# Attention with experts on one core: matrix products in four column groups, another order of the first loads, another router

## The chip, the cores and the metric

The kernel runs on one core of a Trainium2 chip. The metric is the device time of one launch in microseconds, the median of several runs. One further run is recorded by the hardware profiler; its views are called the page (a summary of that execution), the chain of waits (the work that ended last, followed back), the timeline, the groups of instructions and the windows. The engines are called PE (TensorE's matmuls), PEld (its weight loads), DVE (VectorE), ACT (ScalarE), POOL (GpSimd) and SP (SyncE, which here only issues DMAs).

## The reference

Everything is float32. x has the shape (4, 1024, 128): four batches of 1024 tokens of 128 features.

```python
def _L0_attn_ref(x, Wq, Wk, Wv, Wu, rel_bias):       # 8 heads of 16
    ...
    Q, K, V = (silu(Q), silu(K), silu(V))
    scores = jnp.einsum('bhsd,bhtd->bhst', Q, K)
    rel_idx = pos[:, None] - pos[None, :] + MAXLEN - 1
    bias = rel_bias[rel_idx]
    scores = scores + bias.transpose(2, 0, 1)[None]
    scores = scores / jnp.sqrt(jnp.asarray(hd, jnp.float32))
    scores = jnp.where(causal[None, None] == 0, NEG, scores)
    key_mask = jnp.sign(jnp.abs(K).sum(-1))
    scores = jnp.where(key_mask[:, :, None, :] == 0, NEG, scores)
    weights = silu(scores)
    attn = jnp.einsum('bhst,bhtd->bhsd', weights, V)
    ...
    return attn * silu(U)

def _L0_ffn_ref(x, w_gate, w_in, w_out):             # 8 experts, the best 2 are used
    ...
    logits = (xt @ w_gate.T).astype(jnp.float32)
    top_logits, top_idx = jax.lax.top_k(logits, TOP_K)
    top_gates = jax.nn.softmax(top_logits, axis=-1).astype(x.dtype)
    gates = (jax.nn.one_hot(top_idx, E, dtype=x.dtype) * top_gates[..., None]).sum(axis=1)
    for e in range(E):
        h = xt @ w_in[e].T
        y = y + gates[:, e:e + 1] * (h @ w_out[e].T)
    ...

x = x + _L0_attn_ref(_layernorm(x, axis=-1), ...)
x = x + _L0_ffn_ref(_layernorm(x, axis=-1), ...)
```

The weights of attention are silu, not softmax, so no sum over keys is needed. An index of the bias table beyond its end is held at the end, so keys more than 255 tokens back all have the same bias.

## The kernel before

Tokens are handled in blocks of 512 (4 tiles of 128), two a batch, eight in all; the last block is finished in two half groups of 256 tokens. Each step below is a Python generator, and the string ORDER names, letter by letter, which generator takes its next step. No scheduler reorders what follows from it: every engine executes its own instructions in the order in which they were written.

- H, `warm` (L234 to L240): three rounds of products of the identity, whose result is not used.
- K, `constants` (L193): the table `near` of biases by distance, with the causal mask on its diagonal part (L198, L202 on POOL), the far biases copied from `cfar` (L204, on DVE), and small masks.
- P and Q, `prepare` (L289) for the first and the second block of a batch: layernorm, transposed by PE (`layernorm_T`, L255: statistics L262 on DVE, the power L271 and the normalised `xn` L276 on POOL, transposes L283, copy L284). Then keys (L304, with silu into two halves kT, one for even and one for odd heads, L307), queries (L312), the key mask (nz, L318 on DVE, 0/1 products L323, kmask L328), values (L334, silu L339, times the mask L341 on POOL) and the gate U (L351).
- S, `attend` (L355), one unit: scores of 512 columns in all for four pairs of heads (L425), each a product with 32 rows of contraction, in four row groups of the array. DVE adds the near bias (L444), ACT applies silu (L447), or does both for far keys (L452). W, `weigh` (L400), takes the oldest unit that is waiting: products with 128 rows of contraction and 32 output columns (L403), four column groups beside each other, into one accumulator.
- C, D, E, `finish` (L470) for each group of tokens: transposes back (L474), residual, second layernorm, the router's logits (L494, one product a tile: xT is the stationary operand and wgT of 8 columns the moving one; copied out at L496), the choice of the two best and their gates on DVE and POOL (L499 to L534), a transpose of the gates (L542), their way through memory to all partitions (L545, L547 on SP), and gate times x for all experts (L553).
- G, `fold` (L242): w_in and w_out of each expert are multiplied beforehand into one 128x128 matrix (L248).
- X, Y, Z, `experts` (L561): for each tile 8 products accumulated over the experts (L567), residual (L571), store (L607). The last half group uses `experts_then_gates` (L576): products of 512 columns (L585), the gates after.

Except for scores and weighting, a product with a 128x128 stationary operand is one instruction over the whole array (before the compiler's division of each f32 product in two passes). PSUM has a ring of 7 banks (`misc`) and one accumulator for the weighting.

The loads stand at the start (L101 to L148). SP issues both blocks of the first x, the main parts of `near`, `ext` (the bias table with its end repeated, written back to memory, L122), the parts of `near` read from `ext` (L124), the weights of the experts with the other x between. The ACT queue issues the bias table rb, wk, wq, wv, wu, cfar and wgT.

Of the kernel before, what the change touches and what calls it, by code (L numbers as in the profile page):

```python
# [8 lines left out]
F32 = mybir.dt.float32  # L9
BF16 = mybir.dt.bfloat16  # L10
AF = mybir.ActivationFunctionType
# [5 lines left out]
P = 128  # L17
H = 8
# [5 lines left out]
SB = 512  # L24
TPB = SB // P
E = 8
HID = 512
EPS = 1e-5
NEG = -4294967295.0
# [1 line left out]
OFF = -3.0e38  # L31
EULER = 2.718281828459045
RING = 7
LAST = 2


# [2 lines left out]


ORDER = (
    "HHHPPPQQKKKPQPPQQKPQSQKSGGSWSWSGPWPSWWSCPWCSSQWWSCPSQCCPSCWCWPCSCCCWSQGSCWWKCSPPPSWSWSWWCS"
    "WGPSWSWDQSWWSDPGQCWSQQPGQPCCSWSDEQECPPWSQPDSWDWSEGDQEDEDESDWWEDSWQEDSWEWDSXDSWESXSWSWWDSXQ"
    "SEWWSECXECPSWSDEWDWSQPSWDWWDSQYSWWSEEYQPPCSCDSDWCCCESCEWWWCSYQCDSCWSCQYDDCSWWCDWPPQSWSEZQE"
    "SWWSZDCQDSCWDSZCDZCEDDSWDSEEEDWEWSXCSWWCESEWSWSEDDDEXDEXEXDCWDEWSYDCDCCCSCDCCDYCSWDWDCEDDS"
    "CYEYCDSDEEWDWWWDZEEEYYZEZEYEEEEZEYCECCECEEYZYZZZZXZXXX"
)


# [1 line left out]
def preln_silu_attention_moe(  # L51
# [13 lines left out]
    nc = tc.nc  # L65
    B, S, D = x.shape
    NR = rel_biasT.shape[1]
# [15 lines left out]
    def misc():  # L83

        return ps_s.tile([P, SB], F32, tag="bank", name="bank")


    xs = [xpool.tile([P, NT, D], F32, tag="x", name=f"x{b}") for b in range(B)]

# [9 lines left out]
    NPAD = MAXLEN - 1 + TAB  # L99
    FAR = TAB - MAXLEN  # L100
    load_x(0, 0)  # L101
    load_x(0, 1)
    rb = cpool.tile([H, NPAD], F32, tag="rb", name="rb")
    nc.scalar.dma_start(rb[:, NPAD - NR :], rel_biasT)
    wcat = cpool.tile([P, 4, D], F32, tag="wcat", name="wcat")
    for i, w in ((1, wk), (0, wq), (2, wv), (3, wu)):
        nc.scalar.dma_start(wcat[:, i, :], w)
    near = cpool.tile([P, 2, NQ, TAB + P], F32, tag="near", name="near")
    for par in range(2):
        nc.sync.dma_start(  # L110
# [3 lines left out]
                [[1, P], [2 * NR, NQ], [1, MAXLEN]],  # L114
            ),
        )
    nc.vector.tensor_copy(
        rb[:, : NPAD - NR], rb[:, NPAD - NR : NPAD - NR + 1].to_broadcast([H, NPAD - NR])
    )
    gates_d = dpool.tile([B * NB, E, SB], F32, tag="gates_d", name="gates_d")  # L120
    ext = dpool.tile([H, NPAD], F32, tag="ext", name="ext")
    nc.sync.dma_start(ext[:, :], rb)  # L122
    for par in range(2):
        nc.sync.dma_start(  # L124
            near[:, par, :, FAR - P : FAR],
            bass.AP(
                ext.tensor, ext.offset + par * NPAD + FAR - P, [[1, P], [2 * NPAD, NQ], [1, P]]
            ),
        )
    cfar = cpool.tile([P, H], F32, tag="cfar", name="cfar")  # L130
    nc.scalar.dma_start(
        cfar, bass.AP(rel_biasT.tensor, rel_biasT.offset, [[0, P], [NR, H]])
    )
    wgT = cpool.tile([P, E], F32, tag="wgT", name="wgT")
    nc.scalar.dma_start(wgT, w_gateT)
    experts_in = []
    for e0 in range(0, E, 2):
        if e0 in (0, 4):
            load_x(1, e0 // 4)

        if e0 % 4 == 0:
            room = gpool.tile([P, 2, 2, 2, NC, D], F32, tag="wide", name=f"w_in_out_{e0}")
        both = room[:, e0 // 2 % 2]
        for t, w in zip((both[:, 0], both[:, 1]), (w_in, w_outT)):
            nc.sync.dma_start(t, w[e0 : e0 + 2].rearrange("e (c p) d -> p e c d", p=P))
        experts_in.append(both)
    for n in range(2 * NB, B * NB):
        load_x(n // NB, n % NB)  # L148

    def near_of(k, parts):  # L150

# [81 lines left out]

    def warm():  # L234

        for _ in range(3):
            pt = misc()
            for i in range(TPB):
                nc.tensor.matmul(pt[:, i * P : (i + 1) * P], ident, ident, start=True, stop=True)
            yield  # L240

    def fold():  # L242

        for e0, both in zip(range(0, E, 2), experts_in):
            for e in range(2):
                pt = misc()
                for c in range(NC):
                    nc.tensor.matmul(  # L248
                        pt[:, :D], both[:, 0, e, c, :], both[:, 1, e, c, :],
                        start=(c == 0), stop=(c == NC - 1),  # L250
                    )
                nc.scalar.copy(wfold[:, e0 + e, :], pt[:, :D])
                yield
# [35 lines left out]
    def prepare(b, blk):  # L289

        if b not in batches:
            batches[b] = {
                "qT": bpool.tile([P, S], F32, tag="qT", name=f"qT{b}"),
                "kT": bpool.tile([P, 2, S], F32, tag="kT", name=f"kT{b}"),
                "uT": bpool.tile([P, S], F32, tag="uT", name=f"uT{b}"),
                "vp": vps[b % 2],
            }
        qT, kT, uT, vp = (batches[b][n] for n in ("qT", "kT", "uT", "vp"))
        t0 = blk * TPB
        s0 = blk * SB  # L300
        xnT = spool.tile([P, SB], F32, tag="xnT", name="xnT")
        yield from layernorm_T(xs[b][:, t0 : t0 + TPB, :], xnT, "ACT", (b, blk) == (0, 0))
        pt = misc()
        nc.tensor.matmul(pt, wcat[:, 1, :], xnT, start=True, stop=True)  # L304

        for par in range(2):
            nc.scalar.activation(  # L307
                kT[:, par, s0 : s0 + SB], pt, AF.Silu, scale=sel[:, par : par + 1]
            )
        yield  # L310
        pt = misc()
        nc.tensor.matmul(pt, wcat[:, 0, :], xnT, start=True, stop=True)  # L312
        nc.scalar.activation(qT[:, s0 : s0 + SB], pt, AF.Silu)
        yield


        nz = spool.tile([P, SB], BF16, tag="nz", name="nz")
        nc.vector.tensor_tensor(  # L318
            nz, kT[:, 0, s0 : s0 + SB], kT[:, 1, s0 : s0 + SB], ALU.not_equal
        )  # L320
        pt = misc()
        for i in range(TPB):
            nc.tensor.matmul(  # L323
                pt[:, i * H : (i + 1) * H], nz[:, i * P : (i + 1) * P], ones8,
                start=True, stop=True,
            )
        kmask = spool.tile([P, TPB, H], F32, tag="kmask", name="kmask")
        nc.vector.tensor_scalar(  # L328
            kmask.rearrange("p i h -> p (i h)"), pt[:, : TPB * H], 0.0, None, ALU.not_equal
        )  # L330
        yield
        pt = misc()
        for i in range(TPB):
            nc.tensor.matmul(  # L334
                pt[:, i * P : (i + 1) * P], xnT[:, i * P : (i + 1) * P], wcat[:, 2, :],
                start=True, stop=True,
            )
        v = spool.tile([P, TPB, D], F32, tag="v", name="v")
        nc.scalar.activation(v.rearrange("p i d -> p (i d)"), pt, AF.Silu)  # L339
        for par in range(2):  # L340
            nc.gpsimd.tensor_tensor(  # L341
                vp[:, t0 : t0 + TPB, par, :, par, :],
                v.rearrange("p i (k q c) -> p i k q c", k=NQ, q=2)[:, :, :, par, :],
                kmask.rearrange("p i (k q) -> p i k q", q=2)[:, :, :, par]
                .unsqueeze(3)
                .to_broadcast([P, TPB, NQ, HD]),
                ALU.mult,
            )
        yield
        pt = misc()  # L350
        nc.tensor.matmul(pt, wcat[:, 3, :], xnT, start=True, stop=True)  # L351
        nc.scalar.activation(uT[:, s0 : s0 + SB], pt, AF.Silu)
        yield

# [115 lines left out]
    def finish(g, b, t0, nt, gated):  # L470
# [18 lines left out]

        xT = spool.tile([P, nt, P], F32, tag=f"x2T{nt}", name="x2T")  # L490
        yield from layernorm_T(x2, xT.rearrange("p i t -> p (i t)"), "DVE", nt < TPB)
        pt = misc()
        for i in range(nt):
            nc.tensor.matmul(pt[:, i * E : (i + 1) * E], xT[:, i, :], wgT, start=True, stop=True)  # L494
        lg = eight("lg")
        nc.vector.tensor_copy(lg, pt[:, : nt * E].rearrange("p (i e) -> p i e", e=E))  # L496
        yield

        def first_of_largest(v, m, oh, k):  # L499
# [61 lines left out]
    def experts(b, t0, gated):  # L561

        y = spool.tile([P, TPB, D], F32, tag="y", name="y")
        for i in range(TPB):
            pt = misc()
            for e in range(E):
                nc.tensor.matmul(  # L567
                    pt[:, :D], gated[:, e, i * P : (i + 1) * P], wfold[:, e, :],
                    start=(e == 0), stop=(e == E - 1),
                )  # L570
            nc.vector.tensor_tensor(y[:, i, :], pt[:, :D], xs[b][:, t0 + i, :], ALU.add)  # L571
            if i == TPB - 1:
                store(b, t0, TPB, y)
            yield

    def experts_then_gates(b, t0, nt, xT, gates):  # L576
# [3 lines left out]
        for i in range(nt):  # L580
            one = xs[b][:, t0 + i, :]
            gy = spool.tile([P, EH, D], F32, tag="gy", name="gy")
            for e0 in (EH, 0):
                pt = misc()
                nc.tensor.matmul(  # L585
                    pt, xT[:, i, :], wfold[:, e0 : e0 + EH, :].rearrange("p e d -> p (e d)"),
                    start=True, stop=True,
                )
                for e in range(EH):
                    ye = pt[:, e * D : (e + 1) * D]  # L590
# [83 lines left out]
```

## Time and profile before

| what | value |
|---|---|
| median of 4 runs | 291.73 us (291.46 to 291.84) |
| the profiled execution | 291.46 us, of it the span from first to last instruction 289.7 us |
| mean granted TensorE clock | 0.987; 0.5 from 9.2 to 16.1 us after the start |
| first score on PE | 20.39 us |
| start of the last store's work on DVE (L571) | 285.65 us |
| experts' products L567, x448 | 55.1 us busy |
| scores L425, x864, and weighting L403, x864 | 85.6 and 71.9 us busy |
| router L494, x64 | 8.0 us busy |
| moved by DMA | 25.47 MB, 88 GB/s on the mean |

Shares of the span: PE 96%, PEld 55%, DVE 79%, ACT 69%, POOL 36%. The busy time of PE is the time in which some matmul is recorded as under way; matmuls overlap, and their ends are modelled. The starts are the better guide: the chain of waits gives, for each burst of one kind of product, the time until the next burst begins.

### The profile page before, as it was taken

What the parts mean: (1) busy time and instruction counts of PE and PEld (TensorE: products, weight loads), DVE (VectorE), ACT (ScalarE), POOL (GpSimd) and SP (SyncE); (2) the same over time, 40 slices, a digit from 0 to 9 for tenths busy, and PEclk for the clock granted to TensorE, in tenths of its full rate; (3) what the DMA queues carried; (4) which work ended last, traced back from release to release, by engine and by line L of the source; (5) the groups of instructions that cost most, each with busy time, mean ns of one, the idle gap of its engine ahead of it and who ended that gap; (6) DMA issues with size and microseconds to landing.
All of it is one profiled execution on the core that took longest, in us unless ns stands there. A gap on an engine that the chain in (4) does not pass through costs nothing.

```text
span 289.7 us, 6505 instructions
## 1 busy us (share of the span) xinstructions
PE 277.6 (96%) x2591; PEld 160.7 (55%) x2591; DVE 228.7 (79%) x571; ACT 199.2 (69%) x327; POOL 102.9 (36%) x126
## 2 busy tenths in 40 slices
PE   7599999999999999999999999999999999999993
PEld 7255433344445445364653463566676687777873
DVE  3158857688998876879878979887998887797794
ACT  2167999899879778778789787775686683472120
POOL 3812179034207868101134437101702162102251
PEclk9689999999999999999999999999999999999999
DMA  7999000000060000000524200016001702617102
GB/s 187 264 346 329 5 3 1 2 0 3 25 269 0 2 0 3 0 3 0 219 113 181 114 0 0 2 38 276 18 1 40 294 2 75 256 36 294 40 0 72
DMA packets 22061, 25.47 MB, mean 88 GB/s; under 512 B 1952, under 2 KB 21128, under 8 KB 21136
## 3 DMA queue, kind: packets, MB, share of 16 engines
q1 hardware_dynamic: 20256, 24.78, 24.4%
q10 hardware_dynamic: 1776, 0.29, 0.6%
q8 instruction: 20, 0.33, 0.5%
q14 instruction: 9, 0.07, 0.1%
HBM read 22.83 MB, written 2.24 MB: 87 GB/s over the span
## 4 chain that ended last, share of the span: by engine, by line
PE 54%; issue 17%; POOL 17%; DVE 7%; ACT 2%; DMA 1%; POOLq 0%; DVEq 0%
PE bank L425 14%; PE bank L567 14%; PE av L403 12%; POOL xn L276 11%; DVE w L444 5%; POOL rstd L271 4%; PE bank L585 2%; PE bank L494 2%; PE bank L304 2%; POOL vp L341 2%; PE bank L334 2%; PE bank L283 2%; PE bank L312 1%; DMA x<-in_L_attn_x 1%; PE bank L351 1%
## 5 line engine op out<-in xcount | busy, mean ns | idle before, releaser
L444 DVE TENSOR_TENSOR w<-bank,near 128x512 f32<-128x512 f32 (+2 forms) x220 | 116.4, 591 | 22.0 <-PE bank L425 18.5
L447 ACT ACTIVATE w<-w 128x1024 f32<-128x1024 f32 (+2 forms) x110 | 98.3, 913 | 35.5 <-DVE w L444 32.3
L425 PE MATMUL bank<-qT,kT 32*128 32x512 f32 (+3 forms) x864 | 85.6, 481 | 0.0
L452 ACT ACTIVATE w<-bank,cscaled 128x512 f32<-128x512 f32 (+3 forms) x136 | 69.9, 597 | 12.5 <-PE bank L425 12.3
L403 PE MATMUL av<-w,vp 128*32 128x512 f32 (+3 forms) x864 | 71.9, 456 | 0.0
L567 PEld LDWEIGHTS bank<-wfold,gated 128*128 128x128 f32 x448 | 51.9, 192 | 8.1 <-DVE w L444 2.4
L425 PEld LDWEIGHTS bank<-qT,kT 32*128 32x128 f32 x864 | 36.2, 184 | 36.1 <-issue 12.6
L567 PE MATMUL bank<-wfold,gated 128*128 128x128 f32 x448 | 55.1, 279 | 0.0
L276 POOL TENSOR_SCALAR xn<-x,st,rstd 128x128 f32<-128x128 f32 x59 | 51.9, 891 | 1.8
L271 POOL TENSOR_TENSOR rstd<-rs,mhalf 128x4 f32<-128x4 f32 (+1 forms) x17 | 19.0, 1118 | 77.8 <-DVE rs L267 60.7
L403 PEld LDWEIGHTS av<-w,vp 128*32 128x32 f32 x864 | 22.5, 109 | 39.8 <-issue 31.1
L553 DVE TENSOR_TENSOR gated<-gated,x2T 128x1024 f32<-128x1024 f32 x28 | 34.5, 1254 | 0.0
L520 POOL TENSOR_TENSOR ex<-euler,d 128x4 f32<-128x4 f32 (+1 forms) x9 | 11.9, 1322 | 52.8 <-DVE d L518 47.6
L341 POOL TENSOR_TENSOR vp<-v,kmask 128x256 f32<-128x256 f32 x16 | 9.7, 630 | 44.0 <-ACT v L339 44.0
L283 PE MATMUL bank<-ident,xn 128*128 128x128 f32 x64 | 13.0, 297 | 6.0 <-POOL xn L276 5.9
L593 ACT ACTIVATE gy<-bank,gates 128x128 f32<-128x128 f32 x16 | 4.6, 368 | 16.7 <-PE bank L585 10.7
L283 PEld LDWEIGHTS bank<-ident,xn 128*128 128x128 f32 x64 | 7.7, 143 | 12.0 <-POOL xn L276 9.1
L262 DVE BATCH_NORM_STATS2 st<-x 128x6 f32<-128x256 f32 x32 | 12.2, 422 | 0.7 <-DMA x<-in_L_attn_x 0.5
L307 ACT ACTIVATE kT<-bank,sel 128x512 f32<-128x512 f32 x16 | 10.3, 705 | 1.5 <-PE bank L304 1.5
L571 DVE TENSOR_TENSOR y<-bank,x 128x128 f32<-128x128 f32 x28 | 7.8, 284 | 2.9 <-PE bank L567 2.9
L304 PE MATMUL bank<-xnT,wcat 128*128 128x512 f32 x16 | 10.0, 728 | 0.0
L318 DVE TENSOR_TENSOR nz<-kT 128x512 bf16<-128x512 f32 x8 | 5.5, 686 | 5.1 <-ACT kT L307 5.1
(77 smaller groups left out, 212.1 us busy)
## 6 DMA issues: line engine op xcount, KB each, us to landing
gated<-gates_d SPq DMA_DIRECT2D x7, 2048.0 KB, 6.9
x<-in_L_attn_x SPq DMA_DIRECT2D x8, 256.0 KB, 4.4
w_in_out<-in_L_ffn_w_in SPq DMA_DIRECT2D x4, 512.0 KB, 5.6
w_in_out<-in_L_ffn_w_out SPq DMA_DIRECT2D x4, 512.0 KB, 6.0
out<-y SPq DMA_DIRECT2D x7, 256.0 KB, 2.4
near<-in_L_attn_rel_bias SPq DMA_DIRECT2D x2, 512.0 KB, 6.6
near<-ext SPq DMA_DIRECT2D x2, 256.0 KB, 4.2
out<-y SPq DMA_DIRECT2D x2, 128.0 KB, 1.8
```

Of the source, the lines that this page charges most:

```text
L271: nc.gpsimd.tensor_tensor(rstd[:, :nt], rs[:, :nt], mhalf[:, :nt], ALU.pow)
L276: (nc.vector if quick and i != 1 else nc.gpsimd).tensor_scalar(xn[:, i, :], src[:, i, :], st[:, i, 1:2], rstd[:, i : i + 1], ALU.subtract, ...
L283: nc.tensor.transpose(pt[:, i * P : (i + 1) * P], xn[:, i, :], ident)
L304: nc.tensor.matmul(pt, wcat[:, 1, :], xnT, start=True, stop=True)
L341: nc.gpsimd.tensor_tensor(vp[:, t0 : t0 + TPB, par, :, par, :], v.rearrange("p i (k q c) -> p i k q c", k=NQ, q=2)[:, :, :, par, :], kmask ...
L403: nc.tensor.matmul(acc[k * 32 : (k + 1) * 32, nt * P - n : nt * P], vp[:, j, par, k, :, :].rearrange("p q c -> p (q c)"), w[:, k, c : c + ...
L425: nc.tensor.matmul(ps[k][:, c : c + n], kT[k * 32 : (k + 1) * 32, par, j * P : (j + 1) * P], qT[k * 32 : (k + 1) * 32, lo : lo + n], start ...
L444: nc.vector.tensor_tensor(w[:, k, :nn], ps[k][:, :nn], near_of(k, parts), ALU.add)
L447: nc.scalar.activation(w[:, k : k + 2, :nn], w[:, k : k + 2, :nn], AF.Silu, scale=SCALE)
L452: nc.scalar.activation(w[:, k, lo:hi], ps[k][:, lo:hi], AF.Silu, bias=cscaled[:, h : h + 1], scale=SCALE,)
L553: nc.vector.tensor_tensor(wide_g[:, e0 : e0 + 2, :], wide_g[:, e0 : e0 + 2, :], xT.rearrange("p i t -> p (i t)").unsqueeze(1).to_broadcast ...
L567: nc.tensor.matmul(pt[:, :D], gated[:, e, i * P : (i + 1) * P], wfold[:, e, :], start=(e == 0), stop=(e == E - 1),)
```

## The change

1. A helper `product` issues a product as four, each with 32 columns of the stationary operand, into the four quarters of the output's partitions: the form in which the weighting already runs. It replaces the single instruction in warming, fold, keys, queries, the key mask, values, U, the experts' products and `experts_then_gates`. Scores (L425), transposes and weighting stay.
2. The router: wgT is padded with zeros to 32 columns. For a full group of four tiles wgT becomes the stationary operand, and the logits of tile i come out as 32 rows (8 of them used) in column group i; ACT copies this, and one more product with the identity turns it. Half groups keep the old sense with 32 instead of 8 columns.
3. `prepare`: the second silu of the keys stands behind that of the queries.
4. Loads: the second block of the first x goes behind the first part of `near`; `cfar` goes ahead of wq; the parts of `near` from `ext` stand ahead of the experts' weights; the other x are spread among these.
5. ORDER is another string. At its head the steps of the second block no longer come between those of the first: it is `PPHHKKKPKPPKQSPPS` where it was `HHHPPPQQKKKPQPPQQKPQS`. Two rounds of warming are at the head, and the third comes later.

In the compiled program PE has 2495 matmul instructions instead of 1363 (before the division in passes), and changes between its three forms (row groups, column groups, whole array) 161 times instead of 157.

```diff
+GW = 32
...
+    def product(out, stationary, moving, start=True, stop=True):
+        for q in range(0, P, 32):
+            nc.tensor.matmul(
+                out[q : q + 32, :], stationary[:, q : q + 32], moving, start=start, stop=stop
+            )
...
     load_x(0, 0)
-    load_x(0, 1)
     rb = cpool.tile([H, NPAD], F32, tag="rb", name="rb")
     nc.scalar.dma_start(rb[:, NPAD - NR :], rel_biasT)
     wcat = cpool.tile([P, 4, D], F32, tag="wcat", name="wcat")
-    for i, w in ((1, wk), (0, wq), (2, wv), (3, wu)):
+    nc.scalar.dma_start(wcat[:, 1, :], wk)
+    cfar = cpool.tile([P, H], F32, tag="cfar", name="cfar")
+    nc.scalar.dma_start(cfar, ...)
+    for i, w in ((0, wq), (2, wv), (3, wu)):
         nc.scalar.dma_start(wcat[:, i, :], w)
+    wgT = cpool.tile([P, GW], F32, tag="wgT", name="wgT")
+    nc.gpsimd.memset(wgT, 0.0)
+    nc.scalar.dma_start(wgT[:, :E], w_gateT)
...
     for par in range(2):
         nc.sync.dma_start(near[:, par, :, FAR:TAB], ...)
...
+        if par == 0:
+            nc.vector.tensor_copy(rb[:, : NPAD - NR], ...)
+            nc.sync.dma_start(ext[:, :], rb)
         nc.sync.dma_start(near[:, par, :, FAR - P : FAR], ...)
+        load_x(par, 1 - par)
     for e0 in range(0, E, 2):
-        if e0 in (0, 4):
-            load_x(1, e0 // 4)
+        if e0:
+            load_x((e0 // 2 + NB) // NB, e0 // 2 % NB)
...
-        for _ in range(3):
+        for _ in range(HEAT):
             pt = misc()
             for i in range(TPB):
-                nc.tensor.matmul(pt[:, i * P : (i + 1) * P], ident, ident, start=True, stop=True)
+                product(pt[:, i * P : (i + 1) * P], ident, ident)
...
-        pt = misc()
-        nc.tensor.matmul(pt, wcat[:, 1, :], xnT, start=True, stop=True)
-        for par in range(2):
+        def keys(par):
             nc.scalar.activation(
-                kT[:, par, s0 : s0 + SB], pt, AF.Silu, scale=sel[:, par : par + 1]
+                kT[:, par, s0 : s0 + SB], pk, AF.Silu, scale=sel[:, par : par + 1]
             )
+        pk = misc()
+        product(pk, wcat[:, 1, :], xnT)
+        keys(0)
         yield
         pt = misc()
-        nc.tensor.matmul(pt, wcat[:, 0, :], xnT, start=True, stop=True)
+        product(pt, wcat[:, 0, :], xnT)
         nc.scalar.activation(qT[:, s0 : s0 + SB], pt, AF.Silu)
+        keys(1)
         yield
...
-        for i in range(nt):
-            nc.tensor.matmul(pt[:, i * E : (i + 1) * E], xT[:, i, :], wgT, start=True, stop=True)
+        if nt == TPB:
+            for i in range(nt):
+                nc.tensor.matmul(
+                    pt[i * GW : (i + 1) * GW, :P], wgT, xT[:, i, :], start=True, stop=True
+                )
+            across = spool.tile([P, P], F32, tag="across", name="across")
+            nc.scalar.copy(across, pt[:, :P])
+            yield
+            pt = misc()
+            product(pt[:, :P], across, ident)
+        else:
+            for i in range(nt):
+                product(pt[:, i * GW : (i + 1) * GW], xT[:, i, :], wgT)
         lg = eight("lg")
-        nc.vector.tensor_copy(lg, pt[:, : nt * E].rearrange("p (i e) -> p i e", e=E))
+        nc.vector.tensor_copy(
+            lg, pt[:, : nt * GW].rearrange("p (i e) -> p i e", e=GW)[:, :, :E]
+        )
...
             for e in range(E):
-                nc.tensor.matmul(
+                product(
                     pt[:, :D], gated[:, e, i * P : (i + 1) * P], wfold[:, e, :],
                     start=(e == 0), stop=(e == E - 1),
                 )
```

HEAT is 3, as the number before.

## The prediction

> **What bounds the kernel now.** I read the page from its top, then the chain of waits, then the timeline of TensorE in the first 24 us.
>
> ```profile
> PE 277.6 (96%) x2591; PEld 160.7 (55%) x2591; DVE 228.7 (79%) x571; ACT 199.2 (69%) x327; POOL 102.9 (36%) x126
> ...
> PE   7599999999999999999999999999999999999993
> ...
> DVE  3158857688998876879878979887998887797794
> ...
> PEclk9689999999999999999999999999999999999999
> ```
>
> TensorE (PE) is busy in every slice but the first two and the last; VectorE (DVE) has a fifth of the span free. A busy PE may still be waiting, so the pieces of the chain were taken apart: each gives the time of one burst of matmuls up to the next burst. An f32 product is two passes of its columns, hence two records; a burst in four groups has four records for each pass.
>
> ```profile
> 104.11 1.00 PE av L403 x8
> 105.10 1.07 PE bank L425 x8
> ...
> 109.10 1.85 PE av L403 x16
> ...
> 113.50 0.86 PE bank L312 x2
> 114.37 0.79 PE bank L494 x8
> ...
> 116.23 1.86 PE av L403 x24
> ...
> 124.54 1.98 PE bank L567 x16
> ...
> 213.55 3.77 PE bank L567 x32
> ...
> 234.85 5.55 PE bank L567 x48
> ...
> 259.32 3.38 PE av L403 x64
> ```
>
> L403 is the weighting, in four groups of 32 output columns. Its bursts of 2 and 4 passes of 512 columns take 1.00 and 1.85: 0.43 us a pass and 0.14 once. The x24 burst of 1.86 holds two passes of 512, two of 384 and two of 128, the same columns as the x16 burst of 1.85: a pass of 128 columns in this form costs its columns alone, 0.43/4 = 0.1075 us. L567 is the experts' product in the full form: x32 less x16 is 1.79 for 16 passes, 0.1117 us each, and 1.98 leaves 0.19 once. Scores (L425, two passes of 512) take 1.07: 0.21 once. The 512-column products (L312) cost 0.43 a pass in the full form too. The router (L494) has 8 columns a pass and still pays 0.11.
>
> The "once" is paid where the form changes. The compiled order before has 72 bursts of scores, 47 in four groups, and 39 full (8 of these begin with transposes, 0.14): 72x0.21 + 47x0.14 + 31x0.19 + 8x0.14 = 28.7 us. From the first score at 20.39 to the end of the last matmul at 285.1 are 264.7 us, of which columns and changes of form fill 258.0; 6.8 are waits, most of them of the layernorm's transposes for GpSimd's xn. So TensorE's own sum sets the end, with the head ahead of it and 4.6 us of VectorE, ScalarE and store behind.
>
> ```profile
> 1.41 5.04 PE L239 MATMUL bank<-ident 128*128 128x128 f32 x24 [1.41 <-POOL ident masks.py:199]
> ...
> 12.64 3.59 PE L304 MATMUL bank<-xnT,wcat 128*128 128x512 f32 x4
> ...
> 18.43 2.03 PE L334 MATMUL bank<-wcat,xnT 128*128 128x128 f32 x16
> 20.39 1.14 PE L425 MATMUL bank<-qT,kT 32*128 32x512 f32 x8
> ```
>
> In the head, warming (L239) is cover, not work. Keys and queries of both first blocks wait until 12.64, behind the second block's transposes (GpSimd makes that xn until 12.3). Work done by 20.39: 8 transposes 0.9, eight passes of keys and queries 3.4, masks 0.2, values 1.8, together 6.3. So 14.1 us of the head are lost to TensorE.
>
> **The change part by part, on TensorE.**
>
> Experts: 28 bursts of 16 passes, 448 x (0.1117 - 0.1075) = -1.9. Values and fold: 128 passes at the same gain, -0.5. The 512-column products: 0.43 in both forms, nothing.
>
> Changes of form: products now join the weighting's bursts, but the order still goes back to scores, and transposes stand alone. Counted in the compiled order: 71 bursts of scores, 74 in four groups, 17 full, all beginning with transposes. 71x0.21 + 74x0.14 + 17x0.14 = 27.6, so -1.1. The number of changes does not fall (157 to 161), only their price.
>
> Router: for seven groups 8 passes x 0.11 become 2 passes of 128 (gates in rows) and 2 of the product that turns them: 0.89 to 0.43, 7 x -0.46 = -3.2. The two half groups: 4 passes each of 32 columns instead of weight-load-bound 0.11, bounded by 0.027 (32 columns) and 0.11; taken 0.05, -0.5. New work elsewhere: seven ACT copies of 128x128 (0.287 us each, the wfold copy's row), 2.0 us on ScalarE, which is 69% busy. The wait is on the in-order TensorE queue: the turning product stands behind 1 to 4 us of other bursts, the shortest cover being one burst of scores (1.07, near the end); where ScalarE is late, scores and weighting behind it wait too. The sparse read of lg has the same 32 elements: nothing.
>
> Key mask: 4 weight loads and 4 matmuls of 8 columns a block become 16 and 16. No row shows it. Lower bound, all groups beside each other: 0.11; upper bound 32 instructions at the 25 ns between the old matmuls of this line: 0.8; before 0.19. Taken 0.3 (the groups of L403 do overlap): +0.9, between -0.6 and +4.9.
>
> Warming: two rounds at the start instead of three, the third in the fourth fifth of the order: 8 passes, +0.9 at most, nothing if it falls into a wait. Cover lost in the head is treated there.
>
> Sum on TensorE after the head: -1.9 - 0.5 - 1.1 - 3.7 + 0.9 + 0.9 = -5.4.
>
> **The head.** After: the first x lands as before at 3.74, its transposes end at 7.49, ScalarE copies to 8.11. Keys no longer stand behind the second block: four passes of keys and queries from 8.15, 1.7 us at full clock, 3.4 at the half clock that the trace granted from 9.2 to 16.1 us. Then two silu (0.64 and 0.61; the second key half goes behind the queries): first score at 10.6 to 12.3. Next in TensorE's queue is the key mask, which waits for nz, and nz stands in VectorE behind four adds (4x0.61, then 0.69): TensorE idles until 4.3 us after the first score, about 15.8. Work done by then is 0.4 + 1.7 + 0.9 + 0.2 = 3.2, lost 12.6: -1.5. The adds need the near table. Before, its last parts were issued at 10.4 and 10.8 and took 4.2, so 15; in the new order they precede the experts' weights and the second key half's rows go behind one x, so earlier: 12 to 15. If it is 15, the lost part is 15.1, +1.0; if nothing waits, 11, -3.1. Both the second x on the SP queue and wq on ACT's move behind one transfer (0.5 us of issue each); wq lands 5.7 us after its issue, 7.5 before and about 8.1 now, and is wanted at 9.0, so hidden. cfar is issued three places earlier, and VectorE had waited 2.2 us for it: it releases work that has slack. The clearing of wgT puts 0.1 us ahead of ident on GpSimd, hidden since warming ends before the first transposes.
>
> **Waits after the head** are taken as they were, 6.8: between -3 and +6, since VectorE must do the same work in a span 2% shorter (79% to 81%).
>
> Sum: -5.4 - 1.5 = -6.9. The profiled execution has a span of 289.7 in 291.46 us; the median shown is 291.73. So span 282.8, median 284.8.
>
> A rule that speaks against the change: the Trainium skill, "TensorE: Matmul & The Clock Gate", section "Wait — 56ns, not 53.3ns?", says that with hardware decode off each matmul costs the sequencer about 62 ns. By that four matmuls would hold a 128-column pass at 248 ns, and the changed kernel's some 620 new passes of this kind would cost about 87 us more. The trace differs: eight weight loads issued within 0.07 us in this stretch.
>
> ```profile
> 251.77:251.84 0.07, 0.07 (x8) 0.06 (x8) 0.00 (x0) 0.00 (x0) 0.00 (x0) 1.00 0.00 0
> ```
>
> The columns of this view are the busy time of PE, PEld, DVE, ACT and POOL with their instructions. Eight loads and the first four matmuls of this burst start within 0.07 us; at that pace the eight instructions of a pass need under 0.05, less than its 0.1075.
>
> **Rivals.**
>
> 1. Instruction supply (slower). The burst above is short. What the trace holds up for longer is the L403 x64 piece: 128 instructions in 3.38 us, 38 a us, because it asks for no more. A long run of 128-column products asks for 8 in 0.1075, 74 a us, nearly twice that, and the last 7 us are such a run. If the supply holds only 60 a us, a pass takes 0.133 and 620 passes cost 15.8 more: 284.8 + 15.8 = 300.6. It decides from 0.1075 + 6.9/620 = 0.119 us a pass. For it: nothing in the trace asks for that rate. Against: single 128-column passes at full pace, and the 0.07 us window. 9%.
>
> 2. The waits take it (no change to a little faster or slower). VectorE's adds for the first block, now without a second prepared block as cover, and the turning product behind ScalarE. Head +1.0 and waits +5 instead of -1.5 and 0: 284.8 + 7.5 = 292.3 at worst, middle 290. For it: VectorE is at 8 or 9 tenths in most slices. Against: TensorE's slices are full while it is. 18%.
>
> 3. More gain: the head loses only 11 and the waits fall by 3 since block one starts earlier and transposes come better spaced: 284.8 - 1.6 - 3 = 280.2. For it: each wait for xn is a matter of order alone. 11%.
>
> **How the numbers follow.** Forecast 62%, own range 281.5 to 288.5; rivals 9, 18 and 11%. Under 0.2% (0.6 us) a measurement of this kernel cannot tell from no change. Of rival 2 a third is faster, a quarter the same, the rest slower. Faster 0.62 + 0.11 + 0.06 = 0.79; same 0.05; slower 0.09 + 0.07 = 0.16. The range leaves out the supply rival and the edges: 279.8 to 291.5.
>
> **What would show it.** L403's and the experts' bursts at 0.1075 a pass (a burst of 32 passes, 128 records, in about 3.6 us); router bursts of about 0.22; bursts of scores unchanged at 1.07; first score between 10.6 and 12.3, then a gap of some 3 us on TensorE ahead of the key mask; last matmul near 278. Wrong if passes of 128 columns stand over 0.119 apart, if TensorE shows gaps before the turning product, or if it idles in the first block for the near table.

## The result, and the profile after

| | before | after |
|---|---|---|
| median | 291.79 us (291.05 to 292.65, 64 runs) | 292.61 us (291.81 to 293.28, 39 runs) |
| ratio to before, 95% interval | | 1.0025, [1.0018, 1.0031] |
| the profiled execution | 291.46 us, span 289.7 | 291.81 us, span 289.8 |
| first score on PE | 20.39 us | 13.35 us |
| second unit of scores on PE | 22.52 us | 21.20 us |
| end of the last matmul | 285.1 us | 284.5 us |

The change was forecast to save 6.9 us and costs 0.8. The profiled execution of after is its fastest, so of the 0.8 only 0.1 is in the spans of the traces compared below. The page of after:

```profile
PE 274.4 (95%) x4759; PEld 151.6 (52%) x4759; DVE 226.7 (78%) x571; ACT 198.7 (69%) x334; POOL 103.4 (36%) x127
...
PE   6739999999999999999999999999999999999992
...
PEclk9968999999999999999999999999999999999999
```

TensorE is busy 3.2 us less in a span as long as before. Its third slice (14.5 to 21.7 us) has a 3 where before had a 9, and the clock in that slice and the next is at 6 and 8 tenths on the mean. The timeline of TensorE in that stretch (start, us, line and operation, and in brackets the idle time before it and what ended it):

```profile
8.99 3.64 PE L93 MATMUL bank<-xnT,wcat 128*32 128x512 f32 x16 [1.35 <-ACT xnT L297]
13.35 1.14 PE L437 MATMUL bank<-qT,kT 32*128 32x512 f32 x8 [0.72 <-ACT qT L328]
19.16 0.28 PE L93 MATMUL bank<-ones,nz 128*32 128x8 bf16 x16 [4.68 <-DVE nz L334]
19.34 1.94 PE L93 MATMUL bank<-wcat,xnT 128*32 128x128 f32 x32
21.20 2.09 PE L437 MATMUL bank<-qT,kT 32*128 32x128 f32 x16
```

Keys and queries (L93 here is the line inside `product`) take 3.64 us, half pace (1.92 in run 11 below); after one unit of scores TensorE stands for 4.68 us in front of the 0.28 us key mask, and the values and second scores behind it run at the half clock again (granted 0.50 from 18 to 22 us). The chain of waits tells what the key mask stood behind (start, length, what):

```profile
1.28 5.69 DMA near<-in_L_attn_rel_bias
...
6.99 7.11 DMA near<-in_L_attn_rel_bias
...
14.15 0.64 POOL near L211
...
14.85 0.61 POOL near L215
...
16.04 2.48 DVE w L456 x4
18.51 0.61 DVE nz L334
...
19.16 2.11 PE bank L93 x45
```

Two transfers of the near table follow one another, then GpSimd's part of the table and of the key mask's `ones`, then four adds, and only then nz, two thirds of a microsecond of work that had been possible since 14 us. (The adds also needed the first part from `ext`, which landed at 15.90.) The second transfer starts when the first has landed because SP waits. The view of SP's waits (what waited for what, us in total, times, longest), in after:

```profile
SPq L129 <- DMA near<-in_L_attn_rel_bias: 3.0, 1, 3.0
```

And in before:

```profile
SPq L92 <- DMA wcat<-in_L_attn_Wq: 2.2, 1, 2.2
SPq L110 <- DMA x<-in_L_attn_x: 1.4, 1, 1.4
```

So a load also waits for one whose data it does not use (L92 loads x, L110 the second main part of `near`). The issue records in the traces name the semaphore that counts each load's landing: the loads of SP and ACT together take eight of them in turn, and each is issued only after the earlier one with its number has landed. In after both main parts of `near` have number 104; in before the second has 102, that of the first x (landed at 3.75, the part issued at 3.76). Nor is SP's order in the traces that of the source, although "The kernel before" says that no scheduler reorders it: in the source of after a part from `ext` stands between the two main parts, and in the trace both parts from `ext` were issued behind them.

To put numbers on this, each burst in the list of TensorE's instructions was split: its passes at the price of undisturbed bursts, its change of form at the prices of the prediction, and the rest, called waits (time lost to the half clock is in it). The prices leave the split uncertain by some tenths of a microsecond, up to about one between the first row and the waits after 22 us. A burst counts to the row in which it begins. The line before the sum is the time from TensorE's last matmul to the end of the span.

| us | before | after | difference | predicted |
|---|---|---|---|---|
| columns and changes of form, without warming | 264.6 | 258.0 | -6.6 | -6.3 |
| the warming round that came late | | 0.9 | +0.9 | +0.9 |
| waits up to 22 us, with the warming there | 12.5 | 16.0 | +3.5 | -1.5 |
| waits after 22 us | 6.6 | 8.1 | +1.5 | 0 |
| behind the last matmul | 4.6 | 5.3 | +0.7 | 0 |
| sum | | | 0.0 | -6.9 |

### The profile page after: what moved, and what is told of

Same layout as the page of the kernel before. It is cut to its first block, busy times and chain, and to the rows that moved or that the text cites. A ratio compares the mean times of both kernels' runs of the same rounds, so it can differ in the third digit from the quotient of the medians.

```text
span 289.8 us, 10850 instructions
## 1 busy us (share of the span) xinstructions
PE 274.4 (95%) x4759; PEld 151.6 (52%) x4759; DVE 226.7 (78%) x571; ACT 198.7 (69%) x334; POOL 103.4 (36%) x127
## 4 chain that ended last, share of the span: by engine, by line
PE 80%; DVE 8%; DMA 4%; POOL 3%; ACT 3%; issue 1%; SPq 0%; ACTq 0%; DVEq 0%; POOLq 0%
PE bank L93 27%; PE bank L437 26%; PE av L415 22%; DMA near<-in_L_attn_rel_bias 4%; DVE gated L579 3%; PE bank L296 2%; POOL xn L289 1%; ACT w L464 1%; DVE w L456 1%; PE bank L486 1%; ACT w L459 1%; DVE y L620 1%; PE bank L568 1%; DVE y L597 0%; PE bank L508 0%
## 5 line engine op out<-in xcount | busy, mean ns | idle before, releaser
L437 PE MATMUL bank<-qT,kT 32*128 32x512 f32 (+3 forms) x864 | 88.8, 486 | 0.8 <-ACT qT L328 0.7
L415 PE MATMUL av<-w,vp 128*32 128x512 f32 (+3 forms) x864 | 73.4, 455 | 0.0
L437 PEld LDWEIGHTS bank<-qT,kT 32*128 32x128 f32 x864 | 38.4, 186 | 37.0 <-issue 10.5
L93 PE MATMUL bank<-wfold,gated 128*32 128x128 f32 x1792 | 53.8, 274 | 0.2 <-DVE gated L579 0.2
L93 PEld LDWEIGHTS bank<-wfold,gated 128*32 128x32 f32 x1792 | 48.0, 110 | 8.5 <-issue 2.7
L546 POOL TENSOR_TENSOR ex<-euler,d 128x4 f32<-128x4 f32 (+1 forms) x9 | 10.8, 1202 | 54.0 <-DVE d L544 48.1
L93 PE MATMUL bank<-xnT,wcat 128*32 128x512 f32 x192 | 25.6, 635 | 1.3 <-ACT xnT L297 1.3
L353 POOL TENSOR_TENSOR vp<-v,kmask 128x256 f32<-128x256 f32 x16 | 12.8, 819 | 38.4 <-ACT v L351 25.4
L93 PEld LDWEIGHTS bank<-xnT,wcat 128*32 128x32 f32 x192 | 5.8, 115 | 14.2 <-issue 8.1
L318 ACT ACTIVATE kT<-bank,sel 128x512 f32<-128x512 f32 x16 | 11.1, 695 | 2.1 <-PE bank L93 2.1
L296 PE MATMUL bank<-ident,xn 128*128 128x128 f32 x64 | 11.2, 293 | 1.3 <-DVE xn L289 1.0
```

What stands on the lines that cost most here:

```text
L93: nc.tensor.matmul(out[q : q + 32, :], stationary[:, q : q + 32], moving, start=start, stop=stop)
L296: nc.tensor.transpose(pt[:, i * P : (i + 1) * P], xn[:, i, :], ident)
L353: nc.gpsimd.tensor_tensor(vp[:, t0 : t0 + TPB, par, :, par, :], v.rearrange("p i (k q c) -> p i k q c", k=NQ, q=2)[:, :, :, par, :], kmask ...
L415: nc.tensor.matmul(acc[k * 32 : (k + 1) * 32, nt * P - n : nt * P], vp[:, j, par, k, :, :].rearrange("p q c -> p (q c)"), w[:, k, c : c + ...
L437: nc.tensor.matmul(ps[k][:, c : c + n], kT[k * 32 : (k + 1) * 32, par, j * P : (j + 1) * P], qT[k * 32 : (k + 1) * 32, lo : lo + n], start ...
```

## The experiments

All were timed beside the kernel before; ratios are to it.

**1. The products' form alone.** Before, with `product` in all places but scores, transposes and router; loads, order and router stay.

```diff
-                nc.tensor.matmul(
-                    pt[:, :D], gated[:, e, ...], wfold[:, e, :], start=..., stop=...)
+                product(
+                    pt[:, :D], gated[:, e, ...], wfold[:, e, :], start=..., stop=...)
```

> The kernel before with its order, loads and router; only the products (all but scores, transposes and router) are issued in four column groups. Theory H (TensorE's own sum did fall by the form and the router, the changed head gave it back): here the columns shrink by 1.5 us (236.9 instead of 238.4), but products that stood beside transposes and the router now change the form: bursts 72 scores, 79 in groups, 27 full instead of 72, 47, 39, so the changes cost 30.2 instead of 28.7 us. Sum 0: 291 to 292.5 us, ratio 0.997 to 1.003, and 128-column passes at 0.109 us. Rival W (the form itself adds waits all along, by four times the instructions): 294 or more, with gaps between passes. Rival P (my forecast's gain from the products alone): 289.

Measured: 292.88 us, ratio 1.0034 [1.0020, 1.0049]. Columns fall by 1.5 us and changes of form rise by 1.5, as expected; the time, 1.0 above before by the ratio, is a little worse than that sum. In the old order the new form is worth nothing: a full-form burst that stood between two others of its kind now has a change on either side.

**2. The key mask ahead of the first scores.** After, with two steps in ORDER exchanged: the key mask (and nz on VectorE, ahead of the adds) before the first unit of scores.

```diff
-    "PPHHKKKPKPPKQSPPSPQPSG...
+    "PPHHKKKPKPPKQPSPSPQPSG...
```

> The changed kernel with one letter of ORDER moved: the key mask of the first block (P) stands before its first score unit (S). Theory H: TensorE then does mask and values while the near table is still loading; the mask does not wait behind four adds; scores of unit 2 come right behind, so VectorE, which stood still from 19.7 to 23.4 us, goes on. Idle of TensorE before the mask falls from 4.7 us to under 2.5; 288 to 290.5 us. Rival L (the lost time is fixed by loads and later waits, whatever the head's order): 292 to 293.

Measured: 289.96 us, 0.9937 [0.9915, 0.9958], a hit, 2.65 us below after. Its timeline of TensorE:

```profile
15.29 0.28 PE L93 MATMUL bank<-ones,nz 128*32 128x8 bf16 x16 [2.71 <-POOL ones L230]
15.50 2.09 PE L437 MATMUL bank<-qT,kT 32*128 32x512 f32 x8
...
19.39 1.63 PE L437 MATMUL bank<-qT,kT 32*128 32x128 f32 x16
```

The first scores come 2.2 us later than in after and the second 1.8 us earlier: what counts is the second, behind the key mask. The mask now waits for `ones`, which GpSimd makes behind the near table.

**3. The near table's two main parts behind the first x.** After, with the loads in another order (the edit in short).

```diff
     for par in range(2):
         nc.sync.dma_start(near[:, par, :, FAR:TAB], ...)
-        if par == 0:
-            nc.vector.tensor_copy(rb[:, : NPAD - NR], ...)
-            nc.sync.dma_start(ext[:, :], rb)
-        nc.sync.dma_start(near[:, par, :, FAR - P : FAR], ...)
-        load_x(par, 1 - par)
+    nc.vector.tensor_copy(rb[:, : NPAD - NR], ...)
+    nc.sync.dma_start(ext[:, :], rb)
+    for par in range(2):
+        nc.sync.dma_start(near[:, par, :, FAR - P : FAR], ...)
+    for par in range(2):
+        load_x(par, 1 - par)
```

> The changed kernel with another order of the first loads: both main parts of near are issued right behind the first x, and the other x behind. Theory H: the last part of near that the first add waits for lands at 13.5 to 14.5 instead of 15.9, the first add starts so much earlier and about the same is gained: 290 to 291.5 us. Rival (the half clock of TensorE in the head decides, not the near table): first add earlier, time within 0.5 us of 292.6.

Measured: 292.22 us, 1.0025 [1.0007, 1.0043], a miss: the ratio is that of after. The first part from `ext` was issued at 10.32 instead of 8.65 and landed at 15.77 instead of 15.90; the first add came at 15.90 instead of 16.02. Both main parts were now issued without a wait, at 1.29 and 1.83, but the wait moved to `ext`. SP's timeline, then the longest of its waits:

```profile
6.00 0.34 SPq L139 DMA_DIRECT2D ext<-rb  x1
6.58 2.93 SPq L102 DMA_DIRECT2D x<-in_L_attn_x  x2
9.54 0.51 SPq L158 DMA_DIRECT2D w_in_out<-in_L_ffn_w_in  x1
10.32 0.92 SPq L141 DMA_DIRECT2D near<-ext  x2
```

```profile
SPq L139 <- DMA wcat<-in_L_attn_Wk: 3.6, 1, 3.6
```

`ext` was issued at 6.00 (3.64 in after), landed at 10.30 (8.07), and its readers went behind two x and one weight of the experts. So the table did not come earlier, and what an earlier table is worth is not tested by this run.

**4. The loads of before.** After, with the load section of before (wgT padded; part of the edit).

```diff
     load_x(0, 0)
+    load_x(0, 1)
...
-    nc.scalar.dma_start(wcat[:, 1, :], wk)
-    cfar = ...
-    for i, w in ((0, wq), (2, wv), (3, wu)):
+    for i, w in ((1, wk), (0, wq), (2, wv), (3, wu)):
         nc.scalar.dma_start(wcat[:, i, :], w)
+    cfar = ...
```

> The changed kernel with the loads in the order of the kernel before. Theory H (the new order of loads makes near late, 15.9 instead of 14.4): first add near 14.5 to 15, 1 us or so gained, 291 to 292.3 us. Rival (the new loads help, as meant): slower than the changed kernel by 0.5 us or more.

Measured: 291.29 us, 0.9991 [0.9973, 1.0009]: 1.3 below after by the medians, 1.0 by the ratios. The first part from `ext` lands at 14.36, the first add starts at 14.49, the second scores at 19.66. The new order of loads is thus a loss on its own.

**5. Both: old loads, key mask first.** The edits of runs 2 and 4.

> The changed kernel with both edits of the head: the old order of loads and the key mask ahead of the first score unit. Theory H (head lost what TensorE gained): the mask first gave 2.7 us, the old loads 1.3; the first add waits for the near table at 14.4 and for scores that now stand behind the mask at 15.5 to 17.5, so the gains overlap in part: 288 to 289.5 us. Rival (the two gains are one and the same wait): 289.5 to 290.5.

Measured: 290.23 us, 0.9936 [0.9921, 0.9950]. The rival's range: the gains overlap. With the old loads `cfar` comes late, and nz now stood on VectorE behind the copy of it; the mask went at 15.6, no earlier than in run 2.

**6. The same with the third warming round at the head**, and the late one gone.

```diff
-    "PPHHKKKPKPPKQPSPS...        ...EESWHQEW...
+    "PPHHHKKKPKPPKQPSPS...       ...EESWQEW...
```

> As e5_combo, and the third round of warming back at the head instead of late in the order. Theory H: the late round's 0.87 us of matmuls lie in a stretch where TensorE has no gap, so they come off in full; in the head the third round ends at 6.4, when the transposes' input is ready, and lets keys and queries run at the full clock as in the kernel before (passes of 0.43 instead of 0.86 us in part), which brings the first scores up to 1.5 us ahead: 286.5 to 288 us. Rival (the half clock costs nothing, since the near table sets the first add, and the late round fell into a wait): as e5_combo within 0.4 us.

Measured: 290.02 us (286.97 to 290.87), 0.9919 [0.9888, 0.9950]; the median is the rival's. The late round had partly stood in a wait: waits between 200 and 250 us grew by 0.6 when it went.

**7. The old router.** After, with the router's old sense and the full form for all groups (wgT keeps its 32 columns), without the copy and the turning product.

```diff
-                nc.tensor.matmul(
-                    pt[i * GW : (i + 1) * GW, :P], wgT, xT[:, i, :], start=True, stop=True)
-            across = ...
-            nc.scalar.copy(across, pt[:, :P])
-            yield
-            pt = misc()
-            product(pt[:, :P], across, ident)
+        for i in range(nt):
+            nc.tensor.matmul(
+                pt[:, i * GW : (i + 1) * GW], xT[:, i, :], wgT, start=True, stop=True)
+        if nt == TPB:
+            yield
```

> The changed kernel with the router's old sense for all groups (xT stationary over the whole array, wgT moving, now 32 columns), no copy by ScalarE, no turning product; the step keeps its place in ORDER. Theory H (after the head TensorE's sum is the time): columns 236.95 instead of 233.09, and nine more bursts of the full form, changes 30.2 instead of 27.5: +6.6 us, 298 to 300 us. Rival (the router's wait for ScalarE had eaten its gain, or TensorE has slack there): 292 to 295.

Measured: 297.40 us, 1.0186 [1.0173, 1.0199], 4.8 above after; the rival is out, the theory 0.6 too high. Columns and changes rose by 6.6 us as expected, waits fell by 1.0. The groups of TensorE in after show what replaces the 8.0 us of L494 (busy us, mean ns):

```profile
L93 PE MATMUL bank<-ident,across 128*32 128x128 f32 x56 | 2.9, 280 | 0.1
L508 PE MATMUL bank<-x2T,wgT 128*32 128x128 f32 x56 | 2.8, 273 | 0.0
```

The idle time before the turning product is 0.1 us over seven groups: ScalarE's copy was not what TensorE waited for.

**8. The experts in the full form.** After, with the whole-array form in the experts (`experts`) alone.

```diff
-                product(
+                nc.tensor.matmul(
                     pt[:, :D], gated[:, e, i * P : (i + 1) * P], wfold[:, e, :],
```

> The changed kernel with the experts' products (L567 of the kernel before) alone back in the full form. Theory H: 448 passes at 0.1117 instead of 0.1092 and 21 full bursts between the others, columns +1.1, changes 31.2 instead of 27.5: +4.8 us, 296.5 to 298 us. Rival (four times the instructions cost elsewhere what the form saves): 291.5 to 293.

Measured: 293.90 us, 1.0071 [1.0056, 1.0086], 1.3 above after (2.2 by the spans). Below both ranges. Columns and changes did rise by 4.8, but waits fell by 2.2. The chain of waits at the end of this run, and of after, show a further limit:

```profile
269.47 1.80 PE bank L593 x16
271.29 0.29 DVE y L597
```

```profile
267.31 1.93 PE bank L93 x64
269.26 0.29 DVE y L597
```

From here to the end the chain runs over VectorE, ScalarE and GpSimd (the last group's choice of experts, gates and sums), 20.7 us in the one and 20.5 in the other, whatever form the remaining experts' products have.

**9. Run 2 with three warming rounds at the head.** ORDER begins `PPHHHKKKP` and the late H is gone, as in run 6; the loads are after's.

> e2 with the third warming round back at the head and the late one removed (nothing else). Theory (TensorE at half clock in the head, and a late round that costs 0.9 us, are part of what was given back): keys and queries run at full clock, 3.64 us becomes about 2; the key mask still waits for GpSimd's ones at about 15.0; the late round's 0.9 us go, 0.6 of them into a wait: 288.7 to 289.7 against e2's 289.96. Rival (the clock in the head is hidden by the waits for ones and for the near table, and the late round fell into a wait): within 0.4 us of e2, 289.6 to 290.4.

Measured: 290.00 us (289.01 to 291.81), 0.9921 [0.9889, 0.9952]: the rival. In the profiled execution, the slowest of the four, the mask waited 4.17 us for `ones`; keys and queries took 3.22 us there, so the theory's full pace did not come about in it.

**10. Run 2 with `ones` early.** GpSimd makes `ones` ahead of its part of the near table, and wgT is loaded by SP.

```diff
     def constants():
+        nc.gpsimd.memset(ones8, 1.0)
+        nc.gpsimd.affine_select(out=ones8, ...)
+        nc.gpsimd.affine_select(out=ones8, ...)
         for par in range(2):
             diag = near[:, par, :, TAB - P : TAB]
...
-    nc.scalar.dma_start(wgT[:, :E], w_gateT)
...
+    nc.sync.dma_start(wgT[:, :E], w_gateT)
```

> e2 with the key mask's table of ones made on GpSimd ahead of the near table instead of behind it, and the load of wgT moved from ACT's queue to SP's. The key mask then waits for nz alone. Theory (what stands in TensorE's order behind a late operand sets the head): ScalarE's table load and copy come some 0.5 us earlier, the mask at 13.8 to 14.6 instead of 15.29, second scores 0.8 to 1.3 us earlier, 288.7 to 289.4. Rival (the near table sets it: first add not before 15.9, so buffers hold TensorE): 289.6 to 290.4.

Measured: 289.41 us (287.84 to 289.71), 0.9901 [0.9874, 0.9928], on the edge of the theory's range. The mask goes at 13.17, second scores at 17.27 (2.1 us before run 2's); now the first add does wait 2.17 us for the near table, until 15.89. Of the 2.1 us some 1.0 show in the ratios, whose intervals overlap (0.6 in the medians).

**11. Runs 9 and 10 together.** Key mask first, `ones` early, wgT on SP, three warming rounds at the head.

> Both edits of the two runs above. Theory: at full clock keys and queries end near 10, nz near 12, mask near 12.3, first score unit 12.5 to 13.5; first add then waits for the near table at about 15.9, so of these 3 us some 1.5 to 2 come through: 287 to 288.5. Rival (near table): no better than the better of the two runs, 289 to 290.

Measured: 287.22 us (286.51 to 288.39), 0.9841 [0.9816, 0.9866]: the theory's range, 5.4 us below after and 4.6 below before, faster than both. Its timeline of TensorE, then of VectorE:

```profile
8.31 1.92 PE L93 MATMUL bank<-xnT,wcat 128*32 128x512 f32 x16 [0.68 <-ACT xnT L298]
12.98 0.28 PE L93 MATMUL bank<-ones,nz 128*32 128x8 bf16 x16 [2.74 <-DVE nz L335]
13.19 2.09 PE L438 MATMUL bank<-qT,kT 32*128 32x512 f32 x8
...
16.72 1.15 PE L438 MATMUL bank<-qT,kT 32*128 32x128 f32 x16
```

```profile
12.24 0.68 DVE L335 TENSOR_TENSOR nz<-kT 128x512 bf16<-128x512 f32 x1
...
15.35 5.09 DVE L457 TENSOR_TENSOR w<-bank,near 128x512 f32<-128x512 f32 x8 [1.83 <-PE bank L438]
```

Keys and queries run at full pace, the mask goes 6.2 us earlier than in after and the second scores 4.5, and VectorE's first two units of adds are one stretch of 5.09 us where after had 3.7 us of idling between them. By the account of the table the waits up to 22 us, with the warming there, are 11.1, which is 1.4 below before: the size of the -1.5 that the prediction had for the head, by another order of steps than the predicted one. Waits after it are 9.6, 3.0 above before, most of it between 200 and 250 us.

Runs 10 and 11 also start keys and queries 0.7 us earlier, since wgT's load is off ScalarE's queue; how much of the gain that is was not tried by itself.

## Why the prediction was wrong

**TensorE's own sum: right.** Columns and changes of form fell by 6.6 us where 6.3 were predicted. The passes of 128 columns cost 0.109 us each (predicted 0.1075), also in long runs. In after's timeline the 32 passes of this burst end when the next begins, at 272.63:

```profile
269.13 3.68 PE L93 MATMUL bank<-wfold,gated 128*32 128x128 f32 x128
272.63 4.47 PE L93 MATMUL bank<-wfold,x2T 128*32 128x512 f32 x40
```

That is 3.50 us for 128 matmuls, 27 ns each and as many weight loads beside them. So rival 1, the supply of instructions, did not happen. The 62 ns a matmul that the Trainium skill ("TensorE: Matmul & The Clock Gate", section "Wait — 56ns, not 53.3ns?") gives for hardware decode off did not apply here. The key mask, put at +0.9, cost next to nothing: 16 of its matmuls take 0.11 us (from 90.04 in after), 4 in before took 0.10 (from 16.93). That the sum came out is partly luck, since this miss and the price of a pass (some 600 at 0.0015 more, 0.9) have opposite signs. The router is the part that pays (run 7: 4.8 us, while 3.7 and its share in the changes of form were predicted); the form of the other products pays nothing in the old order (run 1) and 1.3 in the new for the experts (run 8), of 4.8 that TensorE's sum says.

**The head: the step that failed.** The prediction put it as "first score at 10.6 to 12.3" and then "TensorE idles until 4.3 us after the first score, about 15.8", so -1.5. The first score came at 13.35, since keys and queries began at 8.99 instead of 8.15 (ScalarE's copy stood behind the issue of wgT's load, which was held until wk had landed at 6.52, 4.69 in before, and a table load) and ran at half pace throughout. But that lateness was not what counted: the 4.3 us put the adds directly behind the scores, and the adds started at 16.02, when the first part of the near table from `ext` had landed at 15.90. The key mask came at 19.16, 3.4 us later than predicted. The prediction saw the table ("12 to 15", because its parts were now issued ahead of the experts' weights); it missed that SP stands 3.0 us at L129 for the first part, so that the second main part was issued at 6.99 (before: 3.76) and landed at 14.09 (before: 10.19). The parts from `ext` were issued earlier, as it said (8.65, before 10.39), but behind that main part, and the first landed later (15.90, before 14.38). The rest is the half clock behind the gap, which the prediction did not count: values and one unit of scores took 1.9 us more than at full pace. Together 3.4 + 1.9 = 5.3, against the 5.0 us between -1.5 and +3.5; the split does not resolve the 0.3.

Undoing the order of these steps, with no change to what is computed or transferred, returned 2.65 us (run 2) and, with `ones` ahead, wgT on SP and the warming, 5.4 us (run 11). Run 4 shows the place of the table in it: where it landed 1.5 us earlier, 1.0 to 1.3 us were won. No run changes the rotation of the semaphores alone.

So rival 2 was right in the place that it named for the head (the first block's adds, "now without a second prepared block as cover"), though its worst time, 292.3, was 0.3 short; that it came so near is partly luck, since the head lost 2.5 more than its bound of +1.0 and the later waits rose by 1.5 where it allowed 5. It was wrong on the turning product, which cost no wait. It had 18%. The order that makes it costly, nz behind four adds, stood in the prediction's own text, and so did a table that lands at 15, for +1.0; with the 1.9 us of half clock behind such a gap that bound would have been some 2.9, and the forecast no longer on the side of a gain in the head.

**Waits after the head: 0 predicted, +1.5 measured.** Run 8 suggests that they answer to TensorE's own speed: 4.8 us more columns, 2.2 us fewer waits; so does run 11, with 3.0 more waits than before at a faster head. The waits for xn in bursts with transposes, which before had (the longest 1.6 us, in the burst from 99.17), are shorter in after; what grew lies in bursts of scores and weighting, in which TensorE is shown as busy (the bursts of scores from 94.60 and 236.31 take 1.0 and 0.8 over their price, and 200 to 250 us in all 1.7 more than in before). Which buffer or engine holds them is not shown and was not tried.

**The end: 0 predicted, +0.7.** Before, the chain of waits stays on TensorE until 281.6; after, it leaves it at 269.3 for the last half group's gates on VectorE. The last 17 us of experts' products are no longer what ends last, so by this chain faster passes there buy nothing; no run changes that stretch alone.

## What to carry to other kernels

A sum over the bounding engine tells what an edit is worth only where that engine stays the bound: here 6.6 us of it were real and all given back: 3.5 in the head, 1.5 in later waits, 0.9 in the late warming round and 0.7 behind the last matmul. When the steps of a second block are taken out from between those of the first, list for each engine's queue what now stands directly behind an operand that lands late, and put small steps that need nothing of it (here nz, `ones` and the key mask, under 2 us) ahead. Do this from the issue times of the transfers in a trace, not from the order of the source, and include what the issuing queue itself waits for.

## What the runs showed of the hardware

- The pace of TensorE in the head differs between the profiled executions. The sixteen records of keys and queries took 3.64 us in after and 1.92 in run 11, as shown above. In run 5, run 10 (both, as after, with two rounds of warming at the head) and run 9 (with three, as run 11):

```profile
7.94 1.93 PE L93 MATMUL bank<-xnT,wcat 128*32 128x512 f32 x16 [0.67 <-ACT xnT L295]
8.32 2.85 PE L93 MATMUL bank<-xnT,wcat 128*32 128x512 f32 x16 [0.67 <-ACT xnT L298]
9.28 3.22 PE L93 MATMUL bank<-xnT,wcat 128*32 128x512 f32 x16 [1.65 <-ACT xnT L297]
```

  The clock records in the traces go with this. Each trace's first record is one of full clock; it begins at 13.2 us in after, 5.9 in run 5, 5.8 in run 10 (until 9.2), 5.1 in run 9 (until 8.5) and 6.1 in run 11 (until 12.9). What ran ahead of the first record ran at half pace: after's two rounds of warming, 16 passes, took 3.64 us, where 0.109 us a pass makes 1.7. A view of the clock shows 1.00 where there is no record, so the 1.00 that it gives in the head of after is no full clock. With three rounds the first record begins between 5.1 and 6.5 us in all five traces (before, runs 1, 6, 9 and 11); with two, between 4.1 and 5.9 in three (runs 5, 7 and 10) and between 12.8 and 24.3 in five. The stretches in the head last 3.4 us or a multiple of it. The Trainium skill ("TensorE: Matmul & The Clock Gate", section "Part 1: The HAM clock gate (the "warmup" mystery)") has the array at half rate until it was busy for about 3.4 us, and again after an idle window, in windows that do not start with the kernel; the rows agree with it.
- Matmuls in four column groups are issued closer together than those over the whole array. Of the key mask's matmuls of 8 columns, 4 over the whole array take 0.10 us (before, 16.93 to 17.03) and 16 in four groups 0.11 (after, 90.04 to 90.15). Of 128 columns, 128 matmuls and as many weight loads take 3.50 us (after, 269.13 to 272.63).
- When a transfer lands is not told by its own issue alone. The first part from `ext` took 4.0 us from issue to landing in before (10.39 to 14.38), 7.2 in after (8.65 to 15.90) and 5.4 in run 3 (10.32 to 15.77). In after the main part ahead of it was issued 3.2 us later than in before, and from 8 to 12 us the DMA moved 140 to 149 GB/s, in before 274 to 288.
